# Four graph layers on one core: the normalisations' reciprocal deviation moved from GpSimd to ScalarE, two of the four normalisations moved from ScalarE to GpSimd, and a new written order

## The chip, the cores and the metric

The kernel runs on one core of a Trainium2 chip. The core has a matrix engine (TensorE, PE in the profile), three engines for elementwise work (VectorE or DVE, ScalarE or ACT, GpSimd or POOL), and DMA queues, here nearly all issued by the fifth engine, SyncE (SP). Each engine works through its own queue in order; an instruction that needs another engine's result waits on a semaphore, and all that is queued behind it on that engine waits with it. The metric is the device time of one execution in microseconds (us), the median of several runs.

## What is computed

The input x holds 32 graphs of 512 nodes with 128 features in float32, and all share one 0/1 adjacency matrix of 512 x 512. Four layers follow each other, each with a residual and a normalisation over the features:

```python
x = _layernorm(x + _L0_gnn_ref(x, adj, ...), axis=-1)   # graph attention, leaky_relu at the end
x = _layernorm(x + _L1_gnn_ref(x, adj, ...), axis=-1)   # graph attention, elu at the end
x = _layernorm(x + _L2_gnn_ref(x, adj, ...), axis=-1)   # A*M @ (x W0) + A*(1-M) @ (x W1) + bias
x = _layernorm(x + _L3_gnn_ref(x, adj, ...), axis=-1)   # ((adj x + x) W + b) / its row norm
# _layernorm(x) = (x - mean) / sqrt(var + 1e-5)
```

An attention layer weights the nodes by a softmax over leaky_relu(e_src[i] + e_dst[j]), masked by the adjacency.

## The kernel before, in words

A graph's 512 nodes lie in four chunks of 128 rows, so a tile of 128 x 512 holds a whole graph, and most steps consist of four instructions on 128 x 128 or one on 128 x 512. A graph goes through some 60 named steps, called units. For the attention of layer k (0 or 1) these are: `ph` (projection on PE, with the attention scalars as three extra columns, line L179), `ex` (Exp of those columns on ACT, L183), `h` (scaling of the projected features on ACT, L189), `rt`, `rw`, `rb` (one scalar per node is transposed on DVE, written to DRAM and read back into all partitions by SP's queue, L214, L220, L224), `al` (the attention matrix: maximum and mask in one DVE instruction for each chunk, L236), `po` (the attention product on PE, L196, the largest single piece of PE's work), `rs` and `v` (division by the row sum), `lr` or `exp` and `elu` (the nonlinearity), `add` (the residual on POOL, L267). Layers 2 and 3 split x into a rounded part and a rest (`xh` on ACT, L273; `xl` on POOL, L277), multiply by a 512 x 512 matrix (`py`, L284), copy out (`y`, ACT L288) and multiply by the weights (`po2` and `po3`, L298 to L311). Layer 3 divides by the row norm: `sq` on ACT, `ssp` on POOL (L325 and L326), `rr` on DVE (L332), which also adds the residual.

Each layer ends in a normalisation of the tile `o`: `bn` takes mean and variance on DVE (L339, L341; the variance comes out with the epsilon in it), and

```python
        @unit(f"pw{k}", f"mv{k}", f"rn{k}")
        def _(b, mv, rn):
            nc.gpsimd.tensor_tensor(rn[:, 0], mv[:, :, 1], mhalf, op=ALU.pow)             # L345
            nc.gpsimd.tensor_mul(rn[:, 1], mv[:, :, 0], rn[:, 0])                         # L346
            nc.gpsimd.tensor_single_scalar(rn[:, 1], rn[:, 1], -1.0, op=ALU.mult)         # L347

        @unit(f"nrm{k}", f"o{k}", f"rn{k}", f"x{k + 1}")
        def _(b, o, rn, xo):
            for c in range(NCH):
                nc.scalar.activation(xo[:, c * P : (c + 1) * P], o[:, c * P : (c + 1) * P],    # L352
                                     AF.Identity, bias=rn[:, 1, c : c + 1], scale=rn[:, 0, c : c + 1])
```

`pw` works on 128 x 4 values (one for each row and chunk), `nrm` on the whole tile. `st` stores the result of layer 3.

Nothing in the kernel decides at run time what comes next. A dictionary `PLAN` gives each unit of each of the 32 graphs a rank, and `STARTS` does so for the setup units. The program is built by sorting all units by rank and emitting them one after the other; each unit's instructions go to the end of their engine's queue. So the ranks are the order in every queue, and some 9 to 17 graphs are under way between their load and their store. Buffers come from fixed stocks (30 tiles of 128 x 512, 6 PSUM banks, 12 small tiles of each kind) and are handed on in rank order: a unit that takes a buffer waits for the last user before it. After the planned part a branch on a flag leads to a general version for unusual inputs, which is not entered here.

Of the kernel before, what the change touches and what calls it, by code (L numbers as in the profile page):

```python
# [15 lines left out]
ALU = mybir.AluOpType  # L16
# [10 lines left out]
def kernel(  # L27
# [300 lines left out]
    @unit("rr", "ss", "x3", "o3")  # L328
    def _(b, ss, x3, o):
        for c in range(NCH):  # L330
            cols = slice(c * P, (c + 1) * P)
            nc.vector.scalar_tensor_tensor(o[:, cols], o[:, cols], ss[:, c : c + 1], x3[:, cols], op0=ALU.mult, op1=ALU.add)  # L332

    for k in range(4):

        @unit(f"bn{k}", f"o{k}", f"st{k}", f"mv{k}")
        def _(b, o, st, mv):
            for c in range(NCH):
                nc.vector.bn_stats(st[:, c, :6], o[:, c * P : (c + 1) * P])  # L339
            for c in range(NCH):  # L340
                nc.vector.bn_aggr(mv[:, c, :], st[:, c, :])  # L341

        @unit(f"pw{k}", f"mv{k}", f"rn{k}")
        def _(b, mv, rn):
            nc.gpsimd.tensor_tensor(rn[:, 0], mv[:, :, 1], mhalf, op=ALU.pow)  # L345
            nc.gpsimd.tensor_mul(rn[:, 1], mv[:, :, 0], rn[:, 0])  # L346
            nc.gpsimd.tensor_single_scalar(rn[:, 1], rn[:, 1], -1.0, op=ALU.mult)  # L347

        @unit(f"nrm{k}", f"o{k}", f"rn{k}", f"x{k + 1}")
        def _(b, o, rn, xo):  # L350
            for c in range(NCH):
                nc.scalar.activation(xo[:, c * P : (c + 1) * P], o[:, c * P : (c + 1) * P], AF.Identity, bias=rn[:, 1, c : c + 1],  # L352
                                     scale=rn[:, 0, c : c + 1])

# [16 lines left out]
    def first():  # L371
# [6 lines left out]
        nc.scalar.activation(bad[:, 0:1], minus1, AF.Exp)  # L378
# [136 lines left out]
    def _(b, p):  # L515
# [3 lines left out]
        "ja": 1, "warm": 2, "wb": 3, "awt0": 4, "e2": 6, "warm2": 7, "awc0": 10, "e0": 11, "e1": 14, "rest": 15,  # L519
        "awq0": 16, "am2": 17, "aws0": 18, "e3": 19, "am0": 20, "eh": 21, "am1": 23, "am3": 26, "m3": 28, "m0": 29,  # L520
        "m2": 31, "m1": 32, "awt1": 36, "mp": 38, "cva2": 39, "cva3": 42, "cvd2": 43, "awc1": 44, "cva1": 47,
        "de": 48, "cvd3": 49, "cva0": 50, "cvd1": 51, "dga": 54, "cvd0": 56, "awq1": 63, "deg": 72, "aws1": 73,
        "lpp": 257, "lpd": 304, "dv": 452, "out_d": 2245, "out_p": 2361, "out_c": 2363,
    }
    PLAN = {
        "ld": [0, 8, 9, 12, 45, 77, 121, 182, 230, 291, 376, 430, 486, 550, 616, 693, 744, 822, 890, 948, 1005, 1070,
            1136, 1211, 1275, 1335, 1401, 1466, 1530, 1585, 1644, 1721],
        "pt0": [5, -1, -1, -1, -1, -1, -1, -1, -1, -1, -1, -1, -1, -1, -1, -1, -1, -1, -1, -1, -1, -1, -1, -1, -1, -1,
            -1, -1, -1, -1, -1, -1],
        "xt0": [13, -1, -1, -1, -1, -1, -1, -1, -1, -1, -1, -1, -1, -1, -1, -1, -1, -1, -1, -1, -1, -1, -1, -1, -1, -1,  # L530
            -1, -1, -1, -1, -1, -1],
        "ph0a": [24, 59, 71, 97, 96, 127, 149, 207, 278, 337, 411, 465, 524, 589, 665, 731, 789, 851, 918, 986, 1045,
            1108, 1177, 1242, 1309, 1370, 1439, 1507, 1568, 1625, 1690, 1751],
        "ph0b": [22, 62, 74, 98, 112, 129, 155, 211, 277, 341, 408, 466, 527, 592, 668, 736, 792, 855, 922, 996, 1047,
            1110, 1178, 1244, 1312, 1371, 1436, 1509, 1589, 1660, 1736, 1816],
        "ex0a": [27, 66, 75, 99, 101, 136, 164, 213, 281, 345, 417, 468, 530, 594, 670, 737, 796, 858, 927, 989, 1054,
            1111, 1182, 1249, 1315, 1373, 1444, 1511, 1575, 1631, 1695, 1757],
        "ex0b": [25, 67, 80, 105, 116, 135, 159, 215, 279, 347, 414, 470, 531, 597, 672, 741, 801, 864, 925, 1003,
            1053, 1116, 1181, 1248, 1320, 1375, 1442, 1517, 1593, 1666, 1743, 1821],
        "pc0": [33, 69, 83, 107, 122, 151, 165, 217, 283, 349, 423, 471, 535, 606, 675, 746, 805, 867, 928, 1012, 1056,  # L540
            1118, 1190, 1256, 1330, 1377, 1455, 1527, 1599, 1669, 1750, 1823],
        "pr0": [34, 68, 81, -1, -1, -1, -1, -1, -1, -1, -1, -1, -1, -1, -1, -1, -1, -1, -1, -1, -1, -1, -1, -1, -1, -1,
            -1, -1, -1, -1, 1805, 1992],
        "h0a": [35, 79, 84, 108, 125, 154, 166, 222, 286, 352, 427, 473, 538, 610, 681, 749, 807, 872, 929, 1015, 1063,
            1124, 1202, 1258, 1338, 1383, 1461, 1529, 1604, 1673, 1758, 1834],
        "h0b": [41, 82, 85, 111, 131, 160, 168, 229, 287, 359, 431, 480, 541, 615, 686, 754, 811, 877, 935, 1020, 1068,
            1128, 1208, 1260, 1346, 1385, 1471, 1534, 1609, 1680, 1762, 1835],
        "al0": [37, 78, 94, -1, -1, -1, -1, -1, -1, -1, -1, -1, -1, -1, -1, -1, -1, -1, -1, -1, -1, -1, -1, -1, -1, -1,
            -1, -1, -1, -1, 1869, 2014],
        "po0a": [46, 88, 104, 172, 188, 202, 243, 290, 360, 416, 500, 529, 596, 660, 739, 818, 892, 971, 999, 1101,  # L550
            1142, 1203, 1319, 1366, 1443, 1513, 1600, 1675, 1755, 1819, 1873, 2034],
        "po0b": [52, 91, 115, 179, 195, 212, 256, 299, 367, 425, 491, 542, 612, 671, 724, 827, 900, 964, 1023, 1115,
            1184, 1253, 1343, 1407, 1474, 1539, 1634, 1724, 1789, 1868, 1888, 2028],
        "rs0a": [53, 93, 118, 185, 200, 225, 253, 302, 377, 426, 508, 543, 611, 667, 751, 830, 911, 990, 1009, 1112,
            1154, 1213, 1342, 1393, 1453, 1525, 1623, 1687, 1766, 1831, 1885, 2044],
        "rs0b": [60, 100, 130, 189, 199, 224, 272, 312, 373, 441, 507, 556, 631, 680, 734, 845, 910, 981, 1032, 1131,
            1195, 1266, 1354, 1417, 1485, 1558, 1647, 1738, 1797, 1874, 1897, 2043],
        "v0a": [55, 102, 120, 187, 203, 247, 255, 309, 382, 433, 510, 547, 621, 674, 756, 846, 917, 992, 1010, 1133,
            1162, 1217, 1355, 1396, 1473, 1532, 1626, 1694, 1771, 1837, 1898, 2049],
        "v0b": [61, 110, 133, 191, 206, 249, 292, 320, 404, 446, 523, 558, 639, 687, 770, 852, 924, 997, 1049, 1135,  # L560
            1200, 1276, 1357, 1431, 1516, 1561, 1653, 1745, 1804, 1899, 1902, 2052],
        "lr": [70, 113, 138, 192, 220, 258, 301, 336, 409, 461, 533, 587, 641, 695, 779, 860, 932, 1002, 1058, 1140,
            1205, 1288, 1361, 1437, 1526, 1571, 1665, 1748, 1815, 1904, 1906, 2063],
        "add0": [76, 117, 144, 197, 226, 261, 311, 344, 413, 464, 537, 618, 652, 703, 788, 870, 942, 1019, 1067, 1148,
            1214, 1294, 1365, 1448, 1541, 1592, 1672, 1753, 1827, 1911, 1915, 2075],
        "bn0": [89, 123, 170, 201, 237, 284, 322, 358, 428, 485, 549, 633, 678, 722, 794, 887, 946, 1027, 1081, 1157,
            1224, 1307, 1388, 1462, 1567, 1606, 1688, 1761, 1833, 1917, 1921, 2080],
        "pw0": [92, 132, 177, 204, 244, 289, 351, 379, 434, 505, 559, 642, 683, 728, 809, 906, 962, 1034, 1100, 1165,
            1230, 1323, 1409, 1469, 1573, 1614, 1696, 1770, 1846, 1938, 1934, 2114],
        "nrm0": [95, 146, 183, 209, 254, 296, 363, 384, 439, 513, 567, 662, 692, 742, 824, 919, 968, 1040, 1145, 1189,  # L570
            1238, 1333, 1415, 1494, 1580, 1637, 1711, 1783, 1862, 1984, 1946, 2124],
        "pt1": [124, 157, 218, 262, 263, 307, 372, 457, 517, 580, 691, 748, 812, 847, 937, 1061, 1150, 1219, 1277,
            1374, 1451, 1531, 1640, 1705, 1760, 1828, 1893, 1937, 1988, 1996, 2083, 2131],
        "xt1": [128, 162, 228, 264, 265, 327, 381, 462, 521, 581, 699, 753, 817, 849, 955, 1066, 1153, 1225, 1282,
            1378, 1458, 1543, 1646, 1709, 1765, 1829, 1900, 1944, 2009, 2035, 2092, 2141],
        "ph1a": [137, 167, 233, 266, 310, 331, 388, 469, 540, 609, 707, 761, 833, 857, 970, 1076, 1161, 1231, 1286,
            1390, 1470, 1546, 1651, 1714, 1776, 1836, 1985, 1947, 2017, 2060, 2097, 2146],
        "ph1b": [134, 169, 231, 267, 314, 333, 397, 472, 552, 605, 709, 759, 835, 879, 980, 1079, 1158, 1228, 1295,
            1386, 1468, 1549, 1650, 1715, 1774, 1839, 1905, 1949, 2015, 2064, 2095, 2149],
# [445 lines left out]
```

## Time and profile before

| | |
|---|---|
| median of 3 runs | 603.15 us (603.14 to 603.32) |
| profiled execution: its own time / its span | 603.0 us / 601.3 us |
| granted TensorE clock, mean | 0.985 |
| PE, DVE, ACT, POOL busy | 554.4, 527.4, 492.7, 461.7 us |
| matmul instructions on PE | 4200 |
| end of the last attention matrix (L236) | 524.0 us |
| start of the last matmul of a graph (L311) | 585.5 us |

A group line reads: line, engine, operation, output <- inputs, shape, count | busy time, mean ns of one | the engine's idle time just before these instructions and what ended it. A wait line reads: who waited <- for whom: us in total, how often, the longest. Busy PE is modelled: a matmul's record is longer than the distance to the next one, so PE's own pace is read from the distance of starts.

### The profile page before, as it was taken

What the parts mean: (1) busy time and instruction counts of PE and PEld (TensorE: products, weight loads), DVE (VectorE), ACT (ScalarE), POOL (GpSimd) and SP (SyncE); (2) the same over time, 40 slices, a digit from 0 to 9 for tenths busy, and PEclk for the clock granted to TensorE, in tenths of its full rate; (3) what the DMA queues carried; (4) which work ended last, traced back from release to release, by engine and by line L of the source; (5) the groups of instructions that cost most, each with busy time, mean ns of one, the idle gap of its engine ahead of it and who ended that gap; (6) DMA issues with size and microseconds to landing.
All of it is one profiled execution on the core that took longest, in us unless ns stands there. A gap on an engine that the chain in (4) does not pass through costs nothing.

```text
span 601.3 us, 13766 instructions
## 1 busy us (share of the span) xinstructions
PE 554.4 (92%) x4200; PEld 515.0 (86%) x4200; DVE 527.4 (88%) x2005; ACT 492.7 (82%) x1525; POOL 461.7 (77%) x706
## 2 busy tenths in 40 slices
PE   7889989999989999899999999999999999999980
PEld 7779979998888998789999989999899799888860
DVE  3989999999989999999999999998996999768574
ACT  4665687787779887699888899899888999987996
POOL 3442597686878787698688789998779988999895
PEclk9989999999989999999999999999999999999996
DMA  7722233332334153233333253231010110100103
GB/s 196 129 72 55 54 72 89 85 78 66 73 72 116 45 122 67 60 74 95 89 98 65 78 124 89 71 89 37 25 48 20 53 37 21 35 2 20 52 20 90
DMA packets 111295, 41.83 MB, mean 70 GB/s; under 512 B 69872, under 2 KB 103792, under 8 KB 111216
## 3 DMA queue, kind: packets, MB, share of 16 engines
q1 hardware_dynamic: 110640, 40.57, 27.5%
q8 instruction: 35, 0.57, 0.4%
q10 hardware_dynamic: 576, 0.33, 0.3%
q14 instruction: 44, 0.36, 0.2%
HBM read 32.38 MB, written 8.50 MB: 68 GB/s over the span
## 4 chain that ended last, share of the span: by engine, by line
POOL 31%; PE 22%; DVE 20%; ACT 13%; DMA 6%; issue 4%; SPq 3%; DVEq 0%; POOLq 0%
PE ps L196 11%; POOL rn L345 10%; ACT sq L352 7%; DVE al L236 7%; POOL sq L267 5%; POOL xr L277 5%; PE ps L284 3%; DVE sq L332 3%; PE ps L179 3%; DVE st L339 3%; POOL sq L292 3%; DMA rb<-rd 2%; POOL ss L326 2%; POOL rn L346 2%; POOL rn L347 2%
## 5 line engine op out<-in xcount | busy, mean ns | idle before, releaser
L196 PE MATMUL ps<-hp,al 128*128 128x129 f32 x2048 | 250.6, 277 | 7.7 <-DVE al L236 4.7
L196 PEld LDWEIGHTS ps<-hp,al 128*128 128x128 f32 x2048 | 240.6, 192 | 14.5 <-ACT hp L189 3.2
L352 ACT ACTIVATE sq<-sq,rn 128x128 f32<-128x128 f32 x512 | 210.7, 490 | 51.4 <-POOL rn L347 51.1
L345 POOL TENSOR_TENSOR rn<-mv,mhalf 128x4 f32<-128x4 f32 x128 | 138.0, 1078 | 36.4 <-DVE mv L341 29.8
L236 DVE SCALAR_TENSOR_TENSOR al<-rb,exps,mp 128x512 f32<-128x512 f32 x216 | 145.7, 735 | 6.3 <-DMA rb<-rd 6.3
L339 DVE BATCH_NORM_STATS2 st<-sq 128x6 f32<-128x128 f32 x512 | 108.9, 273 | 14.0 <-POOL sq L267 14.0
L277 POOL TENSOR_TENSOR xr<-sq,xr 128x512 fp32r<-128x512 f32 x64 | 85.4, 1336 | 5.1 <-ACT xr L273 3.3
L189 ACT ACTIVATE hp<-ps,exps 128x128 f32<-128x128 f32 x256 | 88.4, 419 | 0.1
L179 PE MATMUL ps<-we,sq 128*128 128x131 f32 x512 | 71.6, 280 | 9.7 <-ACT sq L171 3.0
L179 PEld LDWEIGHTS ps<-we,sq 128*128 128x128 f32 x512 | 64.5, 192 | 14.0 <-ACT sq L171 4.4
L284 PE MATMUL ps<-a3t,xr 128*128 128x512 f32 x256 | 67.5, 405 | 0.3 <-DVE sq L243 0.3
L284 PE MATMUL ps<-off,xr 128*128 128x512 f32 x256 | 67.4, 405 | 0.3 <-ACT hp L189 0.3
L332 DVE SCALAR_TENSOR_TENSOR sq<-sq,ss,sq 128x128 f32<-128x128 f32 x128 | 47.3, 430 | 13.5 <-POOL ss L326 13.5
L284 PEld LDWEIGHTS ps<-a3t,xr 128*128 128x128 f32 x256 | 45.7, 189 | 9.8 <-DVE sq L243 0.6
L284 PEld LDWEIGHTS ps<-off,xr 128*128 128x128 f32 x256 | 45.7, 188 | 9.7 <-ACT hp L189 0.8
L298 PE MATMUL ps<-w,sq 128*128 128x128 f32 x256 | 50.3, 278 | 4.0 <-ACT sq L288 3.6
L249 ACT ACTIVATE sq<-ps,rs 128x128 f32<-128x128 f32 x128 | 39.6, 367 | 15.6 <-DVE rs L200 15.6
L267 POOL TENSOR_TENSOR sq<-sq,x 128x512 f32<-128x512 f32 x32 | 41.5, 1300 | 13.2 <-DVE sq L253 11.3
L299 PE MATMUL ps<-w,sq 128*128 128x128 f32 x256 | 49.5, 275 | 0.0
L292 POOL TENSOR_TENSOR sq<-sq,bias_b 128x512 f32<-128x512 f32 x32 | 41.0, 1280 | 10.3 <-ACT sq L352 10.3
L341 DVE BATCH_NORM_AGGREGATE mv<-st 128x2 f32<-128x9 f32 x512 | 48.8, 155 | 0.0
L267 POOL TENSOR_TENSOR sq<-sq,sq 128x512 f32<-128x512 f32 x32 | 41.5, 1297 | 6.5 <-DVE sq L261 6.5
(91 smaller groups left out, 834.3 us busy)
## 6 DMA issues: line engine op xcount, KB each, us to landing
rb<-rd SPq DMA_DIRECT2D x54, 256.0 KB
x<-in_x_dram SPq DMA_DIRECT2D x32, 256.0 KB
out_dram<-sq SPq DMA_DIRECT2D x32, 256.0 KB
sw<-in_x_dram SPq DMA_DIRECT2D x124, 64.0 KB
rd<-rt SPq DMA_DIRECT2D x216, 0.5 KB
an<-in_adj_dram SPq DMA_DIRECT2D x3, 256.0 KB
an<-in_adj_dram ACTq DMA_DIRECT2D x1, 256.0 KB
w<-in_L_gnn_W_dram SPq DMA_DIRECT2D x2, 64.0 KB
```

Of the source, the lines that this page charges most:

```text
L179: nc.tensor.matmul(twos(p)[:, c, :FE], xt[:, (2 * half + c) * P : (2 * half + c + 1) * P], ATT[k], start=True, stop=True)
L189: nc.scalar.activation(h[:, 2 * half + c, :F], twos(p)[:, c, :F], AF.Identity, bias=pc if k else 0.0, scale=pc)
L196: nc.tensor.matmul(twos(p)[:, c, : F + 1], al[:, j, rows], h[:, j, :], start=(j == 0), stop=(j == NCH - 1))
L236: nc.vector.scalar_tensor_tensor(al[:, j, :], r, exps[:, 2 * b + k, 2, j : j + 1], mask[:, j, :], op0=ALU.max, op1=ALU.mult)
L267: nc.gpsimd.tensor_add(o, o, xk)
L277: nc.gpsimd.tensor_sub(xl, xk, xh.bitcast(F32))
L284: nc.tensor.matmul(p, part[:, j * P : (j + 1) * P], mat[:, j, :], start=(i + j == 0), stop=(i + j == NCH))
L292: nc.gpsimd.tensor_tensor(chunks(xb), chunks(x2), bc(bias2_b), op=ALU.add)
L332: nc.vector.scalar_tensor_tensor(o[:, cols], o[:, cols], ss[:, c : c + 1], x3[:, cols], op0=ALU.mult, op1=ALU.add)
L339: nc.vector.bn_stats(st[:, c, :6], o[:, c * P : (c + 1) * P])
L345: nc.gpsimd.tensor_tensor(rn[:, 0], mv[:, :, 1], mhalf, op=ALU.pow)
L352: nc.scalar.activation(xo[:, c * P : (c + 1) * P], o[:, c * P : (c + 1) * P], AF.Identity, bias=rn[:, 1, c : c + 1], scale=rn[:, 0, c : c ...
```

## The change

1. `pw` is removed. In its place `le` takes Ln of the variance and `lx` takes Exp of -0.5 times that, both on ACT and on 128 x 4 values; the result is the reciprocal deviation.
2. For layers 1 and 3 a new unit `nm` forms -mean x deviation in one DVE instruction on 128 x 4, and `nrm` stays on ACT.
3. For layers 0 and 2 the ranks name `nrm0p` and `nrm2p` in place of `nrm0` and `nrm2`: four POOL instructions on 128 x 128, which take mean and reciprocal deviation as per-row scalars. `nm0` and `nm2` are not in the list.
4. `rr` is split into four units `rr0` to `rr3` of one instruction each, so that other DVE work can be put between them.
5. At the start an explicit load of ScalarE's function set number 6 takes the place of a dummy Exp.
6. `STARTS` and `PLAN` are replaced as a whole: 2711 as the highest rank in place of 2423, with all units placed anew.

```diff
-    @unit("rr", "ss", "x3", "o3")
-    def _(b, ss, x3, o):
-        for c in range(NCH):
+    for c in range(NCH):
+
+        @unit(f"rr{c}", "ss", "x3", "o3")
+        def _(b, ss, x3, o, c=c):
             cols = slice(c * P, (c + 1) * P)
             nc.vector.scalar_tensor_tensor(o[:, cols], o[:, cols], ss[:, c : c + 1], x3[:, cols], op0=ALU.mult, op1=ALU.add)
...
-        @unit(f"pw{k}", f"mv{k}", f"rn{k}")
+        @unit(f"le{k}", f"mv{k}", f"rn{k}")
         def _(b, mv, rn):
-            nc.gpsimd.tensor_tensor(rn[:, 0], mv[:, :, 1], mhalf, op=ALU.pow)
-            nc.gpsimd.tensor_mul(rn[:, 1], mv[:, :, 0], rn[:, 0])
-            nc.gpsimd.tensor_single_scalar(rn[:, 1], rn[:, 1], -1.0, op=ALU.mult)
+            nc.scalar.activation(rn[:, 1], mv[:, :, 1], AF.Ln)
+
+        @unit(f"lx{k}", f"rn{k}")
+        def _(b, rn):
+            nc.scalar.activation(rn[:, 0], rn[:, 1], AF.Exp, scale=-0.5)
+
+        @unit(f"nm{k}", f"mv{k}", f"rn{k}")
+        def _(b, mv, rn):
+            nc.vector.scalar_tensor_tensor(rn[:, 1], mv[:, :, 0], -1.0, rn[:, 0], op0=ALU.mult, op1=ALU.mult)
...
+
+        @unit(f"nrm{k}p", f"o{k}", f"mv{k}", f"rn{k}", f"x{k + 1}")
+        def _(b, o, mv, rn, xo):
+            for c in range(NCH):
+                nc.gpsimd.tensor_scalar(xo[:, c * P : (c + 1) * P], o[:, c * P : (c + 1) * P], mv[:, c, 0:1],
+                                        rn[:, 0, c : c + 1], op0=ALU.subtract, op1=ALU.mult)
...
-        nc.scalar.activation(bad[:, 0:1], minus1, AF.Exp)
+        nc.scalar.add_instruction(mybir.InstLoadActFuncSet(name=nc.get_next_instruction_name(), act_func_set_id=6))
```

Of the ranks, the ends of a few rows, before and then after; the last entries are those of the last graphs:

```
al1   ..., 2123, 2196]                                                before
py2   ..., 2125, 2199, 2219, 2236, 2256, 2306, 2300, 2313]
py3   ..., 2176, 2225, 2247, 2286, 2317, 2337, 2355, 2362, 2377, 2386]
al1   ..., 2386, 2471]                                                after
py2   ..., 2403, 2346, 2363, 2509, 2540, 2551, 2573, 2605]
py3   ..., 2476, 2464, 2517, 2612, 2622, 2631, 2643, 2651]
```

The ranks of the first four graphs in the new units of layer 1, after:

```
bn1   201, 256, 403, 483, ...
le1   205, 266, 407, 494, ...
lx1   206, 268, 410, 496, ...
nm1   207, 279, 415, 498, ...
nrm1  209, 283, 419, 501, ...
```

## The prediction, made before the changed kernel ran

> **What bounds the kernel now.** I first read the engines' shares and the chain that ended last.
>
> ```profile
> PE 554.4 (92%) x4200; PEld 515.0 (86%) x4200; DVE 527.4 (88%) x2005; ACT 492.7 (82%) x1525; POOL 461.7 (77%) x706
> ...
> POOL 31%; PE 22%; DVE 20%; ACT 13%; DMA 6%; issue 4%; SPq 3%; DVEq 0%; POOLq 0%
> PE ps L196 11%; POOL rn L345 10%; ACT sq L352 7%; DVE al L236 7%; POOL sq L267 5%; POOL xr L277 5%; PE ps L284 3%; DVE sq L332 3%; PE ps L179 3%; DVE st L339 3%; POOL sq L292 3%; DMA rb<-rd 2%; POOL ss L326 2%; POOL rn L346 2%; POOL rn L347 2%
> ```
>
> POOL is the least busy of the four, yet it holds the largest part of the chain, and 14% of the span (84 us) are the three `pw` lines. So POOL costs latency, not throughput. Throughput is set elsewhere. PE's pace comes from distances of starts: 16 matmuls of L196 take 1.79 us (112 ns each), 8 of L284 take 1.87 us (234 ns). 512 x 234 + 3688 x 112 ns = 533 us. DVE has 527 us. Both are close under the span, and neither loses work by this change. So I cut the span at the end of the last attention matrix (524.0 us) and at the last matmul, and asked for busy time by stage (order: PE, PEld, DVE, ACT, POOL).
>
> ```profile
> 0.00:15.00 15.00, 11.61 (x76) 10.68 (x76) 5.30 (x16) 6.07 (x15) 4.82 (x25) 1.00 0.72 196
> 15.00:400.00 385.00, 364.95 (x2847) 342.84 (x2847) 365.11 (x1312) 310.15 (x971) 284.22 (x427) 0.99 0.35 82
> 400.00:524.00 124.00, 120.67 (x918) 112.06 (x917) 106.50 (x432) 111.40 (x341) 106.57 (x156) 1.00 0.13 37
> 524.00:585.60 61.60, 56.96 (x365) 49.44 (x363) 42.84 (x213) 55.33 (x167) 57.06 (x84) 1.00 0.08 23
> 585.60:601.30 15.70, 0.17 (x2) 0.00 (x0) 7.66 (x39) 9.79 (x35) 9.01 (x17) 0.63 0.30 88
> ```
>
> From 15 to 400 us DVE is the fullest (365.1 of 385, 94.8%). From 400 on it drops to 86% and then 70%, while PE, ACT and POOL are full (97, 90 and 86%, then 92, 90 and 93%). The last 15.7 us have no matmul. Next, who waits:
>
> ```profile
> ACT sq L352 <- POOL rn L347: 51.1, 49, 7.2
> POOL rn L345 <- DVE mv L341: 29.8, 20, 4.1
> DVE st L339 <- POOL sq L267: 14.0, 9, 4.5
> DVE sq L332 <- POOL ss L326: 13.5, 9, 5.7
> ```
>
> ACT's largest wait is for `pw`. DVE waits 27.5 us for POOL.
>
> **POOL's load.** From the groups of POOL:
>
> ```profile
> L345 POOL TENSOR_TENSOR rn<-mv,mhalf 128x4 f32<-128x4 f32 x128 | 138.0, 1078 | 36.4 <-DVE mv L341 29.8 <-DVE rt L214 3.2 <-DVE rs L200 3.1
> L347 POOL TENSOR_SCALAR rn<-rn 128x4 f32<-128x4 f32 x128 | 31.7, 248 | 11.2
> L483 POOL TENSOR_TENSOR sq<-em,ident 128x128 f32<-128x128 f32 x4 | 2.2, 572 | 0.0
> L379 POOL TENSOR_SCALAR nident<-ident 128x128 f32<-128x128 f32 x1 | 0.3, 302 | 0.1
> ```
>
> `pw` removed: 128 x (1078 + 238 for L346 + 248) = 200 us. Added: 64 units x 4 = 256 normalising instructions, which this trace does not show. The same operation on the same shape took 302 ns with constants (L379), with two tensors 572 (L483); on 128x4 it took 248. I take 370, as the operands are one tensor and two scalars: 95 us, ends 63 and 146. POOL: 462 - 200 + 95 = 357 us.
>
> **ACT's load.** 256 instructions of L352 (210.7 us for 512) go: -105 us. 256 small ones come; nearest is L183 on 128x6, 20.9 us for 128, so +42 (ends 14, as starts of L183 lie 55 ns apart at the closest, and 65 with the stall below). ACT: 430. In the new ranks 52 of the 128 Exp follow their Ln with nothing between them on ACT, 49 with one unit. An Exp that waits out its Ln costs up to 180 ns, at most 23 us for all, and free ACT time covers this; without that cover, the PSUM copies queued behind (`h`, `xt`, `y`) come late and PE with them.
>
> **DVE's load.** 64 `nm` on 128x4: the nearest rows are L341 (155 ns, 128x9) and L200 (149); ends 62 (a memset on 128x4, L375) and 244 (L498). At 155: +10 us, ends 4 and 16. The four `rr` stay four instructions.
>
> DVE instructions with two SBUF inputs collide with POOL. `rr`, four instructions at a time, beside three POOL loads:
>
> ```profile
> 302.50 2.58 POOL L277 TENSOR_TENSOR xr<-sq,xr 128x512 fp32r<-128x512 f32 x2
> 302.83 2.92 DVE L332 SCALAR_TENSOR_TENSOR sq<-sq,ss,sq 128x128 f32<-128x128 f32 x4
> ...
> 425.38 1.39 POOL L345 TENSOR_TENSOR rn<-mv,mhalf 128x4 f32<-128x4 f32 x1 [2.00 <-DVE mv L341]
> 425.79 1.13 DVE L332 SCALAR_TENSOR_TENSOR sq<-sq,ss,sq 128x128 f32<-128x128 f32 x4
> ```
>
> Beside the long POOL instruction the four take 2.92 us, beside the power 1.13. L332's mean is 430 ns with a median of 344: 128 x 86 ns = 11 us lost, to 210 us of long POOL instructions (L277, L267, L292). The power is harmless, its successor perhaps not: 95/210 x 11 = 5 us more if the 370 ns pieces hold DVE up as the 1.28 us ones do, 1.5 us if the loss shrinks with their length; the split `rr` could give back 3. I take +1.5, ends -3 and +5.
>
> The Trainium skill, "SBUF — State Buffer", section "Who interferes with whom", says that a DVE instruction with two SBUF inputs and a GpSimd instruction that reads SBUF exclude each other for the whole instruction. The row at 425 us disagrees for the power. By the page the loss would go with all of POOL's time, 357 for 462 us, so 11 us would become 8.5 and the span 4 us less than by my term.
>
> **The small edits.** `STARTS`: the setup's instructions are the same but for a dummy Exp (0.2 us) replaced by an explicit load; the trace has one function load, 1.28 us at the start, beside the input DMAs. SP's DMAs keep their numbers (32 loads, 32 stores, 124 `lb`, 216 `rw`, 54 `rb`); all are ranked anew, and each waits in SP's queue for its producer with later loads behind it. DVE waits 6.3 us in total for `rb`; I leave that, ends -6 and +6.
>
> **The stages summed.** The ranks behind the last attention matrix hold less: 5 `py2` for 7, 7 `py3` for 9, 8 `po3` for 9. PE's work there was 2 x 1.79 (`po1`) + 6 x 0.44 (`pt2`) + 7 x (1.87 + 1.79) + 9 x (1.87 + 0.90) = 56.8 us; now 2 x 1.79 + 5 x 0.44 + 5 x 3.66 + 7 x 1.87 + 8 x 0.90 = 44.4.
> - First stage, now 524.0: DVE has 476.9 us of work. Two layer-2 and two layer-3 passes come forward, 2 x (1.1 + 1.2) for `v2` and `bn2` and 2 x (0.7 + 1.5 + 1.2) for `v3`, `rr` and `bn3`, less one `elu` (0.7) that goes back: 10.7. `nm` brings 8 of its 10 (52 of 64 lie here), collisions 1.5: 497. Head of 15 us with 5.3 busy, the rest at the 94.8% of 15 to 400 us: 15 + 491.7/0.948 = 533.7. DVE's waits for POOL (27.5 us, 21.8 without the one of 5.7 us that ends at 562 us) should shrink with POOL's load; I take 4.7 us here: 529. For PE this is 533 - 44.4 = 489 us of pace in 519 us from its first projection at 9.7 us (94%), against 476 in 514 now (93%).
> - Second stage: 44.4 at the present 92% = 48.3.
> - Third stage: the chain of three small POOL instructions (1.56 us) becomes Ln, Exp, `nm` (about 0.5): 15.7 - 1.1 = 14.6, taken as 14.3 as ACT's 1.8 us wait for it goes too.
>
> 529 + 48.3 + 14.3 = 591.6. Around the span lie 603.0 - 601.3 = 1.7 us: 593.3, and the median is 0.15 above the profiled execution: 593.4. I say 593. The first stage is the uncertain one: 517 if DVE reaches 97% and the 4.7 us go too, 545 if it falls to 92.7% (its mean over 15 to 524, 471.6 of 509): total 581 to 609. The smaller ends above (DVE -9 to +12, DMA -6 to +6) lie inside this.
>
> **Rivals.**
> - *PE alone bounds.* Once POOL is off the chain, PE runs at 98%, as its 400 to 524 us nearly show: 9.7 (first projection) + 533/0.98 + 14 = 568. Against it: from 15 to 400 us DVE stood in front, and still does. 12%.
> - *Cover, no gain.* POOL's chain was one of several equally long, and DVE, with 10 us more, refills the time: at 93.8% the first stage is 539 and the total 603. The stage 15 to 400 us speaks for it. 13%, split over the three outcomes.
> - *Slower: ACT's queue takes the wait over.* Ln stands at the head of ACT's queue until `bn` is done, where POOL stood before (36 us in all, L345). Exp waits for Ln (about 13 us), and `nrm1`, `nrm3` wait for `nm`, which DVE reaches after a median of three other units, some 2 us, while ACT has only two to four units between (64 x 0.4 = 26). That is 75 us of standing, behind which copies out of PSUM queue. ACT gains 63 us of work and 51 of waits, so it decides from about 114 us on, or if the waits fall where PE has no second bank ready: 0.1 us (my estimate) for each of 192 handoffs is 19 us, 612. ACT's 430 us of 590 speak against it. 14%.
> - *Slower: POOL's new instruction is dear.* POOL without it has 262 us; from 1.1 us each it is over DVE's 537. At the power's 1.08 us it has 538 where the forecast has 357, and the late layers queue behind it: as long as the present end at least, 610 by its 93% of 524 to 585 us (538/0.93 + 15 + 15 + 2). L379's 302 ns speaks against it. 3%.
> - *The change is not what it says:* if Ln and Exp don't share a function set, 256 loads of 1.28 us put 328 us on ACT: about 790. The one load named explicitly speaks against it. 2%.
>
> "ScalarE: Activation LUTs" in the Trainium skill, section "Table sets: the hidden batching unit", lists a set with both Ln and Exp, but no run here shows it yet.
>
> **Numbers.** My case has 56%: 581 to 601, on the faster side. 0.2% (1.2 us) is about what a measurement can tell from no change. Faster: 56 + 12 + 3 = 71%. Same: 6%. Slower: 14 + 3 + 2 + 4 = 23%. Range 575 to 609: it leaves out the greater part of the PE case and the tail of the slow ones.
>
> **What would show it.** Right: no L345 `rn`; POOL near 357 and ACT near 430 us; one function load; POOL's normalising at 0.3 to 0.45 us; DVE at 95% until the last attention matrix, that at 517 to 539 us, and some 63 us after it. Wrong: ACT waiting for DVE's `mv` or `rn` over 75 us, `rr` over 430 ns, PE's waits for ACT's copies grown, or over 100 loads of functions.

## The result, and the profile after

The changed kernel takes 624.9 us (median of 4 runs, 623.3 to 625.5) beside 603.14 for the kernel before: 1.0356 times as long, interval 1.0336 to 1.0377. The forecast was 593 us, 1.7% faster; the time came out 3.6% slower, beyond the end of the range at 609. The profiled execution has a span of 621.6 us. Its shares and the head of the chain that ended last:

```profile
PE 562.0 (90%) x4200; PEld 518.5 (83%) x4200; DVE 548.8 (88%) x2069; ACT 430.3 (69%) x1524; POOL 481.5 (77%) x578
DVE 43%; POOL 22%; PE 13%; ACT 12%; issue 6%; DMA 2%; SPq 1%; ACTq 0%; DVEq 0%; POOLq 0%
POOL sq L365 16%; DVE al L236 12%; DVE st L340 10%; DVE sq L333 6%; PE ps L196 5%; ACT sq L359 5%; DVE mv L342 3%; DVE sq L305 3%; POOL sq L267 2%; PE ps L179 2%; DVE sq L253 2%; POOL xr L277 2%; DVE sq L243 2%; DVE sq L261 2%; DVE rn L354 1%
```

ACT came out at 430, as forecast. POOL came out at 481 where 357 was forecast, busier than before the change, and one line of it, the new normalisation L365, holds 16% of the chain; the three `pw` lines that POOL lost had held 14%. The group of that line, and those of the small and the two-input instructions on DVE, with the mean of one behind the comma:

```profile
L365 POOL TENSOR_SCALAR sq<-sq,mv,rn 128x128 f32<-128x128 f32 x256 | 211.8, 843 | 30.9 <-ACT rn L350 10.1 <-DVE st L340 5.4 <-issue 5.1
L333 DVE SCALAR_TENSOR_TENSOR sq<-sq,ss,sq 128x128 f32<-128x128 f32 x128 | 54.2, 468 | 8.3 <-POOL ss L326 8.3
L253 DVE SCALAR_TENSOR_TENSOR sq<-sq 128x512 f32<-128x512 f32 x32 | 28.9, 906 | 0.1
L354 DVE SCALAR_TENSOR_TENSOR rn<-mv,rn 128x4 f32<-128x4 f32 x64 | 16.9, 265 | 2.8 <-ACT rn L350 2.7
```

843 ns stands where I had put 370 and an upper end of 572. By stages, cut at the same two events (order: PE, PEld, DVE, ACT, POOL):

```profile
15.00:400.00 385.00, 358.52 (x2735) 335.36 (x2736) 354.72 (x1293) 258.88 (x923) 297.77 (x351) 0.98 0.34 77
400.00:554.80 154.80, 146.19 (x1109) 135.14 (x1107) 143.23 (x546) 115.83 (x412) 128.22 (x146) 1.00 0.17 45
554.80:606.40 51.60, 45.30 (x278) 37.34 (x279) 36.37 (x166) 37.65 (x136) 46.90 (x51) 1.00 0.05 16
606.40:621.60 15.20, 0.31 (x4) 0.23 (x3) 8.45 (x47) 10.76 (x43) 2.53 (x4) 0.56 0.30 91
```

The last attention matrix ends at 554.8 us instead of 524.0: the whole loss, and more, is in the first stage. The end is shorter, as the ranks had said: 66.8 us behind that point for 77.3. Between 15 and 400 us no engine is full: DVE has 92% where it had 95%, PE 93 for 95. So the time is lost in waiting. Among the waits that are new or grew:

```profile
ACT xr L273 <- POOL sq L365: 46.4, 27, 4.2
ACT rn L346 <- DVE mv L342: 40.3, 36, 4.0
PEld ps L167 <- POOL sq L365: 11.2, 18, 1.2
ACT sq L359 <- DVE rn L354: 8.2, 16, 1.6
```

The longest wait of the first kind in order of time (start, duration, engine and line; in brackets the idle time before):

```profile
264.23 6.62 POOL L365 TENSOR_SCALAR sq<-sq,mv,rn 128x128 f32<-128x128 f32 x8 [2.46 <-ACT rn L350]
...
270.82 1.26 POOL L267 TENSOR_TENSOR sq<-sq,sq 128x512 f32<-128x512 f32 x1
270.89 0.62 ACT L273 CAST xr<-sq 128x512 fp32r<-128x512 f32 x1 [4.19 <-POOL sq L365]
271.41 0.58 ACT L288 COPY sq<-ps 128x512 f32<-128x512 f32 x1
...
272.04 0.49 PE L298 MATMUL ps<-w,sq 128*128 128x128 f32 x2 [1.03 <-ACT sq L288]
...
272.12 0.87 DVE L340 BATCH_NORM_STATS2 st<-sq 128x6 f32<-128x128 f32 x4 [1.73 <-POOL sq L267]
```

Two normalisations, eight instructions, hold POOL for 6.62 us. Behind them in POOL's queue the residual of another graph (L267) is late, and DVE stands 1.73 us for it. On ACT the cast of the normalised tile stands 4.19 us; the copy queued behind it is late, and PE stands 1.03 us for that copy. One slow unit stops three engines, each through the order of its own queue.

### The profile page after: what moved, and what is told of

It reads as the page before. It is cut to its first block, busy times and chain, and to the rows that moved or that the text cites. A ratio compares the mean times of both kernels' runs of the same rounds, so it can differ in the third digit from the quotient of the medians.

```text
span 621.6 us, 13800 instructions
## 1 busy us (share of the span) xinstructions
PE 562.0 (90%) x4200; PEld 518.5 (83%) x4200; DVE 548.8 (88%) x2069; ACT 430.3 (69%) x1524; POOL 481.5 (77%) x578
## 4 chain that ended last, share of the span: by engine, by line
DVE 43%; POOL 22%; PE 13%; ACT 12%; issue 6%; DMA 2%; SPq 1%; ACTq 0%; DVEq 0%; POOLq 0%
POOL sq L365 16%; DVE al L236 12%; DVE st L340 10%; DVE sq L333 6%; PE ps L196 5%; ACT sq L359 5%; DVE mv L342 3%; DVE sq L305 3%; POOL sq L267 2%; PE ps L179 2%; DVE sq L253 2%; POOL xr L277 2%; DVE sq L243 2%; DVE sq L261 2%; DVE rn L354 1%
## 5 line engine op out<-in xcount | busy, mean ns | idle before, releaser
L365 POOL TENSOR_SCALAR sq<-sq,mv,rn 128x128 f32<-128x128 f32 x256 | 211.8, 843 | 30.9 <-ACT rn L350 10.1
L340 DVE BATCH_NORM_STATS2 st<-sq 128x6 f32<-128x128 f32 x512 | 109.1, 273 | 14.3 <-POOL sq L267 14.0
L359 ACT ACTIVATE sq<-sq,rn 128x128 f32<-128x128 f32 x256 | 105.2, 487 | 9.3 <-DVE rn L354 8.2
L179 PE MATMUL ps<-we,sq 128*128 128x131 f32 x512 | 74.1, 282 | 8.5 <-ACT sq L171 2.7
L179 PEld LDWEIGHTS ps<-we,sq 128*128 128x128 f32 x512 | 66.5, 194 | 12.7 <-ACT sq L171 3.7
L273 ACT CAST xr<-sq 128x512 fp32r<-128x512 f32 x64 | 39.3, 620 | 46.4 <-POOL sq L365 46.4
L333 DVE SCALAR_TENSOR_TENSOR sq<-sq,ss,sq 128x128 f32<-128x128 f32 x128 | 54.2, 468 | 8.3 <-POOL ss L326 8.3
L346 ACT ACTIVATE rn<-mv 128x4 f32<-128x4 f32 x128 | 26.3, 206 | 49.6 <-DVE mv L342 40.3
L267 POOL TENSOR_TENSOR sq<-sq,sq 128x512 f32<-128x512 f32 x32 | 42.0, 1314 | 20.1 <-DVE sq L261 14.2
L298 PE MATMUL ps<-w,sq 128*128 128x128 f32 x256 | 50.5, 279 | 5.3 <-ACT sq L288 5.3
L171 ACT COPY sq<-ps 128x512 f32<-128x512 f32 x65 | 37.7, 587 | 23.4 <-PE ps L167 23.4
L167 PE MATMUL ps<-ident,sq 128*128 128x128 f32 x256 | 43.4, 281 | 10.0 <-POOL sq L365 7.5
```

The source lines that it names most:

```text
L179: nc.tensor.matmul(twos(p)[:, c, :FE], xt[:, (2 * half + c) * P : (2 * half + c + 1) * P], ATT[k], start=True, stop=True)
L267: nc.gpsimd.tensor_add(o, o, xk)
L298: nc.tensor.matmul(p[:, cols], y[:, cols], w21, start=True, stop=False)
L365: nc.gpsimd.tensor_scalar(xo[:, c * P : (c + 1) * P], o[:, c * P : (c + 1) * P], mv[:, c, 0:1], rn[:, 0, c : c + 1], op0=ALU.subtract, op1 ...
```

## The experiments

Three theories stood at first. **A**: the price of POOL's new instruction is the loss. **B**: the new list (of ranks, `STARTS` and `PLAN`) is at fault. **C**: Ln and Exp hold up ACT's queue. Theory **D** came after the first four runs: a written list holds good only for the durations it was made for. Beside the experiments the kernel before took 601.4 to 601.6 us, so ratios carry the comparison.

**Back to ACT, in the new list** (e1).

```diff
+    for k in (0, 2):
+        PLAN[f"nrm{k}"] = PLAN.pop(f"nrm{k}p")
+        PLAN[f"nm{k}"] = [t + 0.5 for t in PLAN[f"lx{k}"]]
```

> The new list with the normalisations of layers 0 and 2 back on ACT (nm0 and nm2 right behind lx0 and lx2, nrm0 and nrm2 at the ranks of nrm0p and nrm2p); Ln and Exp stay. Theory A, the price of POOL's new instruction (0.80 us in place of my 0.37, 212 us of POOL): the loss goes with it, 590 to 603 us. Theory B, the new list itself: 612 us or more, since all ranks stay. Theory C, Ln and Exp at the head of ACT's queue: 612 us or more, as they stay too.

Measured: 639.25 us, 1.0634 (1.0594 to 1.0673), as B and C had said. A miss for A in the form in which I had put it: taking POOL's instruction away by giving ACT its work back (ACT 524 us, POOL 272) is no cure. The run did not undo the price alone; it changed two engines' load against the list.

**A cheaper instruction in the same places** (e2).

```diff
-    tensor_scalar(x, o, mean, deviation, op0=ALU.subtract, op1=ALU.mult)
+    k == 0: tensor_scalar(x, o, deviation, 1.0, op0=ALU.mult, op1=ALU.mult)       # L369
+    k == 2: tensor_scalar(x, o, 0.0, 1.0, op0=ALU.subtract, op1=ALU.mult)         # L367
```

> The changed kernel with a cheaper instruction in the same places: layer 0 only multiplies by the deviation (one per-row scalar, one constant), layer 2 subtracts 0 and multiplies by 1 (two constants), so the tiles are not normalised. It gives the price of the form: if per-row scalars are what is dear, layer 2 shows about 0.30 us, layer 0 something like 0.55, and none of 0.80. Theory A: POOL falls by 90 to 110 us, 588 to 603 us in all, which is my prediction with its assumed price. Theory B and C: 612 us or more.

Measured: 589.06 us, 0.9800 (0.9764 to 0.9837). POOL's groups:

```profile
L367 POOL TENSOR_SCALAR sq<-sq 128x128 f32<-128x128 f32 x128 | 82.0, 665 | 1.0
L369 POOL TENSOR_SCALAR sq<-sq,rn 128x128 f32<-128x128 f32 x128 | 46.1, 377 | 19.6 <-ACT rn L350 16.0 <-issue 3.1
```

A held, and my guess on the form did not: the form with two constants was the dear one, the form with a per-row scalar the cheap one. They differ in `subtract`. Layer 2 here no longer waits for Exp, which e12 below settles.

**Ln and Exp alone, in the old list** (e3).

```diff
-            nc.gpsimd.tensor_tensor(rn[:, 0], mv[:, :, 1], mhalf, op=ALU.pow)
-            nc.gpsimd.tensor_mul(rn[:, 1], mv[:, :, 0], rn[:, 0])
-            nc.gpsimd.tensor_single_scalar(rn[:, 1], rn[:, 1], -1.0, op=ALU.mult)
+            nc.scalar.activation(rn[:, 1], mv[:, :, 1], AF.Ln)
+            nc.scalar.activation(rn[:, 0], rn[:, 1], AF.Exp, scale=-0.5)
+            nc.vector.scalar_tensor_tensor(rn[:, 1], mv[:, :, 0], -1.0, rn[:, 0], op0=ALU.mult, op1=ALU.mult)
```

> The old list and all normalisations on ACT, only the power and the two small POOL instructions replaced at their place by Ln, Exp and one DVE instruction. Theory A: this part alone does no harm, 596 to 605 us (POOL 262 us, ACT 530). Theory C, Ln standing at the head of ACT's queue until DVE's statistics are there: 610 us or more, with ACT's waits for mv and rn above the present 51 us.

Measured: 633.6 us, 1.0539 (1.0500 to 1.0578). A missed and the time is in C's range: in this setting Ln, Exp and the DVE instruction cost 32 us. But the waits named by C are not the mark of it: ACT's wait for `mv` is 22.4 us and that for `rn` 14.0, together less than the 51 us before. What grew is on the engines that wait for ACT (the first was 22.5 us before):

```profile
POOL hp L204 <- ACT exps L183: 77.6, 38, 7.0
...
DVE rn L347 <- ACT rn L346: 40.7, 41, 3.3
```

**The old units in the new list** (e4): the power at the ranks of `le`, all normalisations on ACT.

> The units of the kernel before in the new list: power and its two followers on POOL at the ranks of le, all normalisations on ACT. Theory B, the list: 615 us or more. Theory A: 598 to 612 us, near the time before, though the list was not made for these units. Against e1 it gives what Ln and Exp are worth in the new list.

Measured: 649.88 us, 1.0798 (1.0753 to 1.0843). The units of the kernel before lose 48 us in the other list. Taken alone this would speak for B; with e2, where the same list gives 589, it speaks for D.

**The full computation with mult and add** (e6).

```diff
-                                        mv[:, c, 0:1], rn[:, 0, c : c + 1], op0=ALU.subtract, op1=ALU.mult)
+                                        rn[:, 0, c : c + 1], rn[:, 1, c : c + 1], op0=ALU.mult, op1=ALU.add)
+    for k in (0, 2):
+        PLAN[f"nm{k}"] = [t + 0.5 for t in PLAN[f"lx{k}"]]
```

> The changed kernel, whole computation and same list, with POOL's normalisation written as mult by the deviation and add of -mean x deviation in place of subtract and mult; nm0 and nm2 on DVE stand right behind lx0 and lx2 (64 more DVE instructions, about 10 us of DVE). Theory A, now as the form of the instruction: it costs 0.38 to 0.45 us as the mult form did (0.377), POOL falls to about 370 us, and the time is 588 to 600 us, my prediction's own case. If two per-row scalars are dear in themselves: 0.6 us or more, and 600 to 620 us. Theory B, the list: over 612 us.

Measured: 601.06 us, 0.9996 (0.9979 to 1.0012), no difference from the kernel before. The instruction fell to 478 ns, POOL to 390 us, and still the time is 8 us over the forecast and just outside A's 588 to 600. The 64 added instructions on DVE are the cause, as e10 below takes 587 us without them (their group, and POOL's wait for it):

```profile
L354 DVE SCALAR_TENSOR_TENSOR rn<-mv,rn 128x4 f32<-128x4 f32 x128 | 36.8, 291 | 8.4 <-ACT rn L350 8.0
...
POOL sq L365 <- DVE rn L354: 40.4, 30, 2.9
```

`nm` has a median of 160 ns and a mean of 291, because it too has two SBUF inputs and meets POOL's long instructions: the 35 of 128 that overlapped a 128 x 512 TENSOR_TENSOR of POOL by more than 50 ns took 643 ns on average, the 65 that overlapped no such instruction, no normalisation and no power 151. And POOL now waits 40 us for DVE.

**The same units in the old list** (e7).

> The old list with the same units: Ln, Exp and nm at the place of the power, layers 0 and 2 normalised on POOL by mult and add. ACT is freed as in the changed kernel, but the list is the old one. Theory A: the units matter, the list little: 590 to 603 us. Theory D, a written list holds good only for the durations it was made for (as the old units lost 47 us in the new list): 605 to 625 us.

Measured: 638.93 us, 1.0624 (1.0591 to 1.0658). The same units (only `rr` is not split here) take 601 us in one list and 639 in the other. That is D, by more than the 605 to 625 that I had said.

**A table of prices** (e8): four forms in layer 0, four in layer 2.

> A table of prices, all else as in e6: each of the four POOL instructions of layer 0 has another form (subtract-mult, add-mult, mult-subtract, mult-add, each with two per-row scalars), and so in layer 2 (add-mult with two constants, mult-add with two constants, subtract alone, mult alone with a per-row scalar), so the tiles are not normalised. If subtract as an operation is dear: the forms with subtract cost 0.65 to 0.8 us, the others 0.3 to 0.45. If the first place decides (anything but mult there): add-mult costs as much as subtract-mult, and mult-subtract is cheap.

Measured: 600.29 us in a single run, and one form for each line (ns: least / median / longest). In order: subtract-mult, add-mult, mult-subtract, mult-add with two per-row scalars; add-mult and mult-add with constants; subtract alone and mult alone with one per-row scalar.

```profile
L370 POOL TENSOR_SCALAR sq<-sq,mv,rn x32: 796/802/1305, 26.6 to 501.4; 128x128 f32<-128x128 f32 x32
L371 POOL TENSOR_SCALAR sq<-sq,mv,rn x32: 438/446/470, 27.4 to 502.7; 128x128 f32<-128x128 f32 x32
L372 POOL TENSOR_SCALAR sq<-sq,rn x32: 797/805/1177, 27.8 to 503.1; 128x128 f32<-128x128 f32 x32
L373 POOL TENSOR_SCALAR sq<-sq,rn x32: 443/452/654, 28.6 to 503.9; 128x128 f32<-128x128 f32 x32
L375 POOL TENSOR_SCALAR sq<-sq x32: 294/300/454, 78.9 to 574.9; 128x128 f32<-128x128 f32 x32
L376 POOL TENSOR_SCALAR sq<-sq x32: 294/300/728, 79.2 to 575.2; 128x128 f32<-128x128 f32 x32
L377 POOL TENSOR_SCALAR sq<-sq,mv x32: 602/612/1033, 79.4 to 575.4; 128x128 f32<-128x128 f32 x32
L378 POOL TENSOR_SCALAR sq<-sq,rn x32: 599/605/1036, 80.0 to 576.0; 128x128 f32<-128x128 f32 x32
```

`subtract` in either place costs 800 ns, `add` in either place 450. Two per-row scalars in place of constants cost 150 ns (446 against 300). The two prices add: subtract-mult with two constants had a median of 642 ns in e2, 340 over mult-add with constants and 160 under subtract-mult with per-row scalars. A single operation is dearer than a pair (605 for mult alone, where e2's mult-mult with one per-row scalar took 372), and alone subtract costs no more than mult (612).

**A dose** (e9): layer 0 with subtract-mult, layer 2 with mult-add and `nm2`.

> A dose: layer 0 keeps subtract and mult (0.80 us), layer 2 has mult and add (0.38 to 0.45) with nm2 on DVE. Theory A: the loss goes with the number of dear units, about half of it left: 603 to 612 us. If only one of the layers carries the loss (layer 0 sits before the second attention, layer 2 before the last matrix): near 593 or near 622.

Measured: 609.62 us, 1.0137 (1.0107 to 1.0166). Between e6 (601) and the changed kernel (625), and inside A's 603 to 612, so by this run the loss is no matter of one layer alone.

**One word** (e12).

```diff
-                                        rn[:, 0, c : c + 1], op0=ALU.subtract, op1=ALU.mult)
+                                        rn[:, 0, c : c + 1], op0=ALU.add, op1=ALU.mult)
```

> The changed kernel with one word edited: the four POOL instructions add the mean in place of subtracting it, so layers 0 and 2 are not rightly normalised; list, waits and all other instructions are the same. By the table of forms 0.45 us each in place of 0.80, POOL falls by about 90 us to 390. Theory A: 588 to 597 us, as without the dear form. If e2 owed its 589 us to the wait on Exp that its layer 2 had dropped: 600 us or more.

Measured: 586.41 us, 0.9762 (0.9726 to 0.9797), against 1.0356 for the changed kernel. This is the cleanest of the runs: same list, same waits, same number of instructions. Its shares and chain, the stages from 15 us on (cut at 521 and 569 us, close to the same two events), and the group of L365 with two groups that wait for POOL:

```profile
PE 546.9 (94%) x4200; PEld 511.8 (88%) x4200; DVE 546.0 (94%) x2069; ACT 430.7 (74%) x1524; POOL 386.2 (66%) x578
DVE 67%; PE 12%; ACT 9%; issue 5%; POOL 3%; DMA 2%; SPq 1%; ACTq 0%; DVEq 0%; POOLq 0%
```

```profile
15.00:400.00 385.00, 371.59 (x2916) 350.56 (x2916) 377.54 (x1391) 279.14 (x1000) 253.27 (x376) 1.00 0.35 82
400.00:521.00 121.00, 117.16 (x915) 111.09 (x914) 114.14 (x445) 94.11 (x329) 85.02 (x120) 1.00 0.14 40
521.00:569.00 48.00, 46.61 (x296) 39.98 (x294) 40.01 (x172) 39.69 (x140) 39.20 (x52) 1.00 0.07 20
```

```profile
L365 POOL TENSOR_SCALAR sq<-sq,mv,rn 128x128 f32<-128x128 f32 x256 | 115.2, 465 | 39.5 <-ACT rn L350 16.2 <-DVE st L340 6.3 <-issue 5.5
L273 ACT CAST xr<-sq 128x512 fp32r<-128x512 f32 x64 | 39.2, 620 | 8.8 <-POOL sq L365 8.6
L340 DVE BATCH_NORM_STATS2 st<-sq 128x6 f32<-128x128 f32 x512 | 109.1, 274 | 2.0 <-POOL sq L267 1.9
```

POOL has 95 us less, the span 38 us less, and DVE is full from 15 to 400 us (377.5 of 385, 98%) and holds 67% of the chain. The waits go with the price: the cast on ACT stands 8.6 us for the normalised tile where it stood 46.4, and DVE stands 1.9 us for the residual of L267 where it stood 14.0. The granted clock was 0.975 in the changed kernel, 0.988 here and 0.985 before; as only the operation was edited, the lower clock follows from the price too, and what it is worth by itself the runs don't separate.

**The whole computation at the cheap price** (e10).

```diff
             nc.scalar.activation(rn[:, 1], mv[:, :, 1], AF.Ln)
+            if k % 2 == 0:
+                nc.scalar.activation(mv[:, :, 0], mv[:, :, 0], AF.Copy, scale=-1.0)
...
-                                        rn[:, 0, c : c + 1], op0=ALU.subtract, op1=ALU.mult)
+                                        rn[:, 0, c : c + 1], op0=ALU.add, op1=ALU.mult)
```

> The whole computation with the cheap form: ACT negates the mean in place by a small Copy (128 x 4) between Ln and Exp of layers 0 and 2, and POOL adds it and multiplies; no nm0 and nm2 on DVE, same list. Theory A: ACT has the room (431 of 600 us busy), 588 to 598 us, faster than both kernels. If e6's 601 us came from the form and not from DVE's 64 extra small instructions (18 us lost to collisions) and POOL's wait for them: about 600 us again.

Measured: 587.16 us, 0.9782 (0.9742 to 0.9822): faster than both kernels. The group of POOL's normalisation (L367 here):

```profile
L367 POOL TENSOR_SCALAR sq<-sq,mv,rn 128x128 f32<-128x128 f32 x256 | 115.9, 467 | 40.6 <-ACT rn L352 14.3 <-issue 6.8 <-DVE st L340 6.2
```

The 64 Copies take 196 ns each on ACT, and the trace shows no engine waiting for them.

**`nm` off DVE** (e11): as e10, with the Copy in all four layers, and

```diff
-            nc.vector.scalar_tensor_tensor(rn[:, 1], mv[:, :, 0], -1.0, rn[:, 0], op0=ALU.mult, op1=ALU.mult)
+            nc.gpsimd.tensor_mul(rn[:, 1], mv[:, :, 0], rn[:, 0])
```

> As e10, and nm1 and nm3 too leave DVE: ACT negates the mean in all four layers, POOL multiplies it by the deviation (128 x 4, about 0.22 us, 64 times). DVE loses about 20 us of work (nm with its collisions). If DVE is the bound of what is left: 575 to 588 us. If POOL's queue gives it back, as nm now waits for Exp there with long instructions around it: 588 to 600 us.

Measured: 580.76 us, 0.9657 (0.9621 to 0.9693), the fastest version here.

```profile
PE 546.5 (94%) x4200; PEld 512.3 (88%) x4200; DVE 533.0 (92%) x2005; ACT 437.8 (75%) x1652; POOL 398.3 (69%) x642
```

DVE lost 12 us of work against e10 (545 to 533) and the time fell by 6. This fits DVE as a bound of what is left, though not the only one.

## Why the prediction was wrong

**The term that failed** is POOL's price: "I take 370 ... 95 us, ends 63 and 146". It measured 212 us of busy time (843 ns each). I chose the nearest row by the operation's name and shape (L379, 302 ns). But L379 multiplies and adds two constants, and the new instruction subtracts and multiplies with per-row scalars. The table of prices splits the distance from L379: 150 ns for the per-row scalars, which I had partly allowed for, and 350 for `subtract`, which I had not; the mean of 843 lies another 44 over the median of 799. The upper end of 572 was the row of another operation, not a bound. A step of the first stage fell with it, that DVE would wait less for POOL, for which I had taken 4.7 us off: of 27.5 us, 21.8 of them in that stage, 22.3 are left (14.0 for the residual, 8.3 for `ss`). At the price of e12 4.1 are left.

**The rival that named it was right in the term, and wrong in how it costs and from what size.** "POOL's new instruction is dear" had 3%, and was to decide "from 1.1 us each", where POOL's sum would pass DVE's, with the late layers queueing behind it. It decided at 0.84 us, with POOL at 481 us under DVE's 549, and before the last attention matrix, not at the end. An engine's sum need not be the largest to set the time: between 0.465 (e12) and 0.843 us (changed kernel) the time went from 0.976 to 1.036 of the kernel before, with POOL never over 77% busy. What counts, by the waits that came and went with the price, is how long a unit holds its queue while others stand behind it. Which duration the list's author had in mind the runs don't show. They show only that the list works at 0.465 us and not at 0.843.

**Near the assumed price the forecast was near, in part by luck.** e12 and e10 took 0.976 and 0.978 of the kernel before; 593 of 603.14 is 0.983. Stage by stage, e12 against the sum: last attention matrix at 522.7 us (529 forecast), from there to the last matmul 45.9 (48.3), the end 15.3 (14.3). So cutting by the last attention matrix and counting what the ranks leave behind it was sound. The luck is in the first stage, where two misses had opposite signs: DVE's collisions, and how full DVE can be. Ranks 5, 7 and 8 in place of 7, 9 and 9 did shorten the end in the changed kernel too.

**DVE's collisions were under-sized, and it did not matter as I thought.** I took +1.5 us. From the groups after (mean less median, `rr` 342, `lr` 679, `nm` 152 ns): 128 x 126 + 32 x 227 + 64 x 113 = 31 us, for 11 of `rr` and 2 of `lr` before. I had not seen that `nm` itself has two SBUF inputs and so collides; its 155 ns were right as a median. But e12 has the same collisions (`rr` 471 ns, `nm` 343) at 586 us: there DVE made up for them by being busy 98% from 15 to 400 us instead of the 94.8% I had carried over. "`rr` over 430 ns", which I had listed as a mark of failure, marks nothing.

The rule that I had weighed, "SBUF — State Buffer" in the Trainium skill, "SBUF: two separate sides" and "Who interferes with whom" (a DVE instruction with two SBUF inputs and a GpSimd instruction that reads SBUF exclude each other for the whole instruction), fits the long two-tensor instructions, not this one: in the changed kernel 40 `rr` overlapped L365 by more than 50 ns and took 376 ns on average, 31 overlapped one of the 128 x 512 two-tensor POOL instructions and took 859 (one `rr` of 1375 ns met both and is in both counts), the rest 338. So the new instruction costs DVE little by collisions; it costs through POOL's queue.

**ACT's queue** was not the cause. The waits of the slower rival did come: before Ln 40.3 us for `mv` and 8.1 for other DVE work, and 8.2 for `nm`. But e12 keeps most of them (32.8, 11.7 and 10.2) and is fast; ACT is idle there for 153 us of the span. e3 shows the rival's other side: with all normalisations left on ACT (532 us busy) and in the old list, Ln, Exp and `nm` cost 32 us.

**The function set** held. The changed kernel has one load, which took 1.3 us. "ScalarE: Activation LUTs" in the Trainium skill, "Table sets: the hidden batching unit", says so of a set with both Ln and Exp.

**The list.** I treated the ranks mostly as neutral. With the units that it was written for, near the assumed price, that did no harm. e4, e7 and e1 show what other units do in a list: old units in the new list 1.080, new units at the cheap price in the old list 1.062, all normalisations on ACT in the new list 1.063. Each is a larger loss than the change itself.

## What to carry to other kernels

Before pricing an instruction by a row of the profile, compare the arithmetic operation and the kind of each operand, not only the name, engine and shape; where no row matches, the nearest row is no upper end. In a kernel with a written order, test a suspected price by editing that instruction alone and leaving the list as it is: experiments that move work between engines (e1, e3) answer another question. And a duration in such an order can matter long before the engine is full: here POOL was busy 77% of the span.

## What the runs showed of the hardware that I had not expected

On POOL, a TENSOR_SCALAR of 128 x 128 in float32 takes 300 ns for mult and add with constants, 450 with two per-row scalars, and 605 for a single mult with one per-row scalar. Where one of two operations is a subtract it takes some 350 ns more: 642 with constants, 800 with two per-row scalars. With two per-row scalars, subtracting cost nearly twice what adding did. Why is open: no run shows what POOL does inside an instruction.
